# A Perceiver layer with 32 routed experts: six instead of eight experts with weights loaded ahead of routing, eight instead of seven blocks shared by 96 and 32 rows

## The chip, the cores and the metric

The kernel runs on one core of one Trainium2 chip. The time is device time in microseconds (us) of one execution of the whole program; lower is better. PE is the matrix engine (TensorE), DVE the vector engine, ACT the scalar engine, POOL is GpSimd, and SP the engine whose only work here is to issue DMAs. PEld is the loading of weights into PE. All arithmetic is in float32.

## The reference, cut to what matters

The layer takes 256 rows of 512 numbers and a context of 4096 rows, and adds three parts to the rows, one after the other: attention over the context (16 heads, 4 of keys and values), a state-space part with a convolution of width 4, and a mixture of experts. The last is what the change touches:

```python
x = hidden_states.reshape(-1, HID)                   # 256 x 512, layer-normed rows
scores = jax.nn.sigmoid(x @ gate_w)                  # 32 experts
topk_w, topk_i = jax.lax.top_k(scores, 6)
topk_w = topk_w / (jnp.sum(topk_w, axis=-1, keepdims=True) + 1e-20)
combine = jnp.sum(jax.nn.one_hot(topk_i, 32) * topk_w[..., None], axis=1)
g = jnp.einsum('td,edf->tef', x, wg)                 # wg, wu: 32 x 512 x 192
u = jnp.einsum('td,edf->tef', x, wu)
act = jax.nn.silu(g) * u
routed = jnp.einsum('tef,efd,te->td', act, wd, combine)   # wd: 32 x 192 x 512
shared = silu(hidden_states @ sg) * (hidden_states @ su) @ sd
return routed + shared
```

Each of the 256 rows is sent to 6 of 32 experts: 1536 pairs of row and expert, 48 for an expert in the mean. How many rows an expert really gets is known only when the program has run the first two parts and the router.

## The kernel before, in words

The program is written with a framework that puts instructions on the engines, finds dependences through tiles, and itself orders the instructions of each engine (a scheduler that knows estimated durations; `tc.issue_after(x)` holds instructions back until x). Attention and the state-space part come first and take about 780 us. What follows here is the expert part.

**Pairs and blocks.** The 32 experts are worked through in 16 pairs (`NP`, n = 0 to 15). A block is 128 rows for PE. A pair is of one of three kinds:

- n below `NW` (two blocks): each expert has a block of 128 rows of its own. `gate_up` (L1672 and on; its matmuls are in the helper at L237) makes gate and up for both with 16 matmuls, `turn_hidden` (L1690) transposes the hidden values (three transposes), and `down` (L1700, L1703) makes the result.
- the next `MIXED` pairs (one block): a large and a small expert share one block, 96 rows and 32 rows.
- the rest (one block): two experts share a block, 64 rows each.

For the one-block kinds `gate_up_two` (L1629) issues matmuls on column groups of 32 or 64 rows, each with the weights of the expert whose rows they are; `turn_hidden_two` (L1641) has two transposes and `down_two` or `down_here` (L1651, L1652) one result.

**Who gets which room.** The first `FIXED` experts keep their numbers: expert 2n and 2n+1 are pair n, whatever the routing says. The others are sorted by their count of rows on the chip, in `places` (L1250): the `WIDES` largest get full blocks, the next `MIXED` ones 96 rows, then come those with 64, and the smallest get 32 (tables made by `place_tables`, L1189). So for each place behind the fixed ones a table `place` says which expert sits there. If an expert has more rows than its room, `crowded` is 1 (`room`, L1341), and a long path (the Else branch behind L1818) computes all experts again in full; the short path only adds and stores the result.

**Weights.** An expert pair's weights are two tiles (gate, up and most of down) and a third with the rest of down, 2.36 MB together. There are `NHELD` = 6 places for a pair's weights in SBUF, made from tiles of the earlier parts as these come free (`hold`, L1420). Fixed pairs are loaded from `hold` as plain DMAs of SP, before routing (L1402 to L1407). The other pairs need `place`, so they are loaded after routing with indirect DMAs of POOL (L1394, called at L1410 to L1412), the first ones, up to pair 5, in this loop:

```python
for n in range(FIXED // 2, NHELD):
    with tc.issue_after(begun):
        begun = load_pair(n)
```

and pair n + 5 in round n, after `down(n - 1)` has freed its place.

**Rows.** The layer-normed rows lie in DRAM (`xd`). `fetch` (L1394 with `xg_sb`) gets a block's rows by an indirect DMA of POOL with the lists in `listed`; the lists of the first `EARLY` = 4 blocks are made ahead by `list_early`, those of the others by `list_later` (L1314, after gate and up of pair 0). `turn` transposes a block's rows on PE (L1601) and copies them on DVE (`xgT`, L1603).

**A round** n issues, in this order in the code: gate and up of n, fetches of blocks up to 4 ahead, `turn(n + 1)`, `down(n - 1)`, `load_pair(n + 5)`, `turn_hidden(n)`. In round 2 `weights_back` (L1716 to L1740) is called: a chain of some 40 small DVE instructions and ten transposes of PE (`spreadT`, L1739) that prepares the routing weights of the last `TAIL` = 10 experts. The results of the first pairs, up to n = 10, go to DRAM (`ye`) and are gathered again for each row (`yk`, 12 indirect DMAs) and added by DVE (L1565); those of the last five pairs are kept in SBUF and spread to their rows by PE (`total`, L1670).

The derived numbers, which the change moves:

```python
NW = (FIXED + WIDES) // 2
NSLOT = NE - FIXED
NB = FIXED + WIDES + (NSLOT - WIDES) // 2
NPL = NSLOT + NSLOT // 2
ZROW = (NW + LAST) * P
```

With FIXED = 8 and MIXED = 7 there are 5 pairs of two blocks (four fixed ones and the two largest of the rest), 7 of 96 and 32 rows, 4 of 64 and 64: NB = 21 blocks.

Of the kernel before, what the change touches and what calls it, by code (L numbers as in the profile page):

```python
# [53 lines left out]
WGU = KD * 2 * FE  # L54
WEX = WGU + DM
NHELD = 6
FIXED = 8
HALFP = P // 2
QUARTER = P // 4
WIDES = 2  # L60
MIXED = 7
HEAD = 4
EARLY = 4
TAIL = 10
NW = (FIXED + WIDES) // 2
LAST = NP - TAIL // 2
# [3 lines that stand above are left out]
# [4 lines left out]
def first_rows(n):  # L74
    return P - QUARTER if n < NW + MIXED else HALFP

# [8 lines left out]
def perceiver_layer(ctx: ExitStack, tc: tile.TileContext, a: dict, out: bass.AP):  # L85
# [64 lines left out]
    def layer(ctx, bounded):  # L150
# [1024 lines left out]
        def routing_memory():  # L1175
# [9 lines left out]
            V.tensor_scalar(m["free"], ident[:, 0:NE], 1.0, None, ALU.mult)  # L1185
            V.memset(m["free"][:, 0:FIXED], 0.0)
            V.tensor_tensor(m["before"], upper, ident, ALU.subtract)

        def place_tables():  # L1189
# [4 lines left out]
            def steps(to, first, *by):  # L1194
                to = to if len(by) == 1 else to.rearrange("p (a b) -> p a b", b=by[1][1])
                G.iota(to, pattern=[list(b) for b in by], base=first, channel_multiplier=0, allow_small_or_imprecise_dtypes=True)

            turn, rows, room, w = m["turn"], m["table"][:, 0], m["table"][:, 1], WIDES + 2 * MIXED
            for to, at0, step, more, narrow in ((turn, 0, 1, NSLOT - MIXED - WIDES, 1), (rows, FIXED * P, P, P - QUARTER, HALFP)):
                steps(to[:, 0:WIDES], at0, (step, WIDES))  # L1200
                steps(to[:, WIDES:w], at0 + WIDES * step, (step, MIXED), (more, 2))
                steps(to[:, w:NSLOT], at0 + (WIDES + MIXED) * step, (narrow, NSLOT - w))
            steps(room[:, WIDES:w], QUARTER, (0, MIXED), (P - HALFP, 2))
            V.tensor_scalar(rows[:, NSLOT:], m["p"], float(P), None, ALU.mult)
# [45 lines left out]
        def places(pc):  # L1250

            pos, key, keys, at, value, drawn = (
                m[n] for n in ("pos", "key", "keys", "at", "value", "dst"))
            n, low = NSLOT, slice(FIXED, NE)
            two = lambda ap, k: ap.unsqueeze(1).to_broadcast([P, 2, k])
# [655 lines left out]
```

## Time and profile before

| | us |
|---|---|
| three timed runs | 940.9, 940.94, 943.85 |
| their median | 940.94 |
| the profiled execution | 946.23 |
| its span, from first to last instruction | 944.3 |
| first fetch of rows (POOL) | 801.85 |
| first gate and up matmuls (pair 0) | 810.04 |
| last instruction group of PE (`total`) ends | 937.9 |

The page of a profile gives the busy time of each engine, then the span in 40 slices, DMA queues, and the chain of work that ended last: followed back from the last instruction, at each step to whatever released it. The share of an engine in that chain says how much of the time hangs on it. Answers of the trace give single rows: start, duration, engine, line, operation, the tiles, and in brackets how long the engine had been idle and who released it. "Landed" is the time at which a DMA's semaphore is counted up. The granted clock of PE is 1.00 where PE runs at full speed; the mean of this execution is 0.997.

### The profile page before, as it was taken

What the parts mean: (1) busy time and instruction counts of PE and PEld (TensorE: products, weight loads), DVE (VectorE), ACT (ScalarE), POOL (GpSimd) and SP (SyncE); (2) the same over time, 40 slices, a digit from 0 to 9 for tenths busy, and PEclk for the clock granted to TensorE, in tenths of its full rate; (3) what the DMA queues carried; (4) which work ended last, traced back from release to release, by engine and by line L of the source; (5) the groups of instructions that cost most, each with busy time, mean ns of one, the idle gap of its engine ahead of it and who ended that gap; (6) DMA issues with size and microseconds to landing.
All of it is one profiled execution on the core that took longest, in us unless ns stands there. A gap on an engine that the chain in (4) does not pass through costs nothing.

```text
span 944.3 us, 10567 instructions
## 1 busy us (share of the span) xinstructions
PE 924.2 (98%) x3266; PEld 504.9 (53%) x3266; DVE 577.4 (61%) x1199; ACT 370.0 (39%) x853; POOL 427.8 (45%) x498
## 2 busy tenths in 40 slices
PE   7999999999999999999999999999999999999996
PEld 3444555555555555555555555554465775654332
DVE  4866766566666665756666656658588685661224
ACT  4556444344344343443444434434154442022121
POOL 3769846345544644724725544220013251545542
PEclk9999999999999999999999999999999999999999
DMA  9651053053024114204305203090025481779983
GB/s 331 203 112 58 1 179 89 1 154 92 1 66 146 33 31 159 57 3 154 90 0 157 68 1 89 14 298 1 0 101 197 145 309 68 288 287 348 421 330 101
DMA packets 129716, 122.33 MB, mean 130 GB/s; under 512 B 79889, under 2 KB 99122, under 8 KB 124402
## 3 DMA queue, kind: packets, MB, share of 16 engines
q1 hardware_dynamic: 118960, 77.43, 27.2%
q0 software_dynamic: 7504, 39.59, 11.3%
q10 hardware_dynamic: 3186, 4.54, 1.3%
q8 instruction: 28, 0.46, 0.2%
q14 instruction: 38, 0.31, 0.1%
HBM read 89.54 MB, written 32.00 MB: 129 GB/s over the span
## 4 chain that ended last, share of the span: by engine, by line
PE 96%; DVE 2%; DMA 0%; issue 0%; ACT 0%; POOL 0%; SPq 0%; ACTq 0%
PE oT L774 24%; PE scT L748 24%; PE ps_kv L522 16%; PE ps_self L237 4%; PE ps_egu L1629 3%; PE ps_o L969 3%; PE ps_egu L237 3%; PE ps_first L399 3%; PE ps_xbc L237 2%; PE ps_out L1163 1%; PE ps_z L237 1%; PE xgTp L1601 1%; PE ps_ye L1651 1%; PE ps_ye L1652 1%; PE total L1670 1%; PE ps_ye L1700 1%
## 5 line engine op out<-in xcount | busy, mean ns | idle before, releaser
L765 DVE TENSOR_TENSOR lacc<-lacc,prT 128x512 f32<-128x512 f32 x256 | 199.8, 781 | 198.0 <-ACT prT L754 196.6
L754 ACT ACTIVATE prT<-scT,bq,rk 128x512 f32<-128x512 f32 x256 | 198.4, 775 | 280.9 <-PE scT L748 268.8
L748 PE MATMUL scT<-qT,kT 128*128 128x512 f32 x536 | 273.5, 592 | 0.0
L774 PE MATMUL oT<-prT,v 128*128 128x512 f32 x528 | 269.4, 592 | 0.0
L774 PEld LDWEIGHTS oT<-prT,v 128*128 128x128 f32 x528 | 100.2, 190 | 125.3 <-issue 118.6
L748 PEld LDWEIGHTS scT<-qT,kT 128*128 128x128 f32 x536 | 101.3, 190 | 41.4 <-issue 30.8
L522 PE MATMUL ps_kv<-fast,ctx 128*128 128x256 f32 x350 | 99.5, 379 | 0.0
L522 PEld LDWEIGHTS ps_kv<-fast,ctx 128*128 128x128 f32 x350 | 66.5, 190 | 47.9 <-issue 39.9
L471 POOL TENSOR_TENSOR ctx<-ctx 128x128 f32<-128x128 f32 x21 | 10.4, 495 | 98.7 <-PE ps_kv L522 98.7
L211 POOL TENSOR_TENSOR rk<-pv,mhalf 128x4 f32<-128x4 f32 x32 | 38.7, 1219 | 27.3 <-DVE pv L210 27.1
L522 PE MATMUL ps_kv<-wkv,ctx 128*128 128x256 f32 x168 | 48.8, 379 | 0.0
L282 ACT ACTIVATE xn<-kraw 128x128 f32<-128x128 f32 x112 | 33.5, 301 | 38.5 <-POOL kraw L497 21.5
L507 POOL TENSOR_TENSOR v<-fast,v 128x768 f32<-128x768 f32 x21 | 40.8, 1958 | 16.5 <-DVE fast L551 15.9
L522 PEld LDWEIGHTS ps_kv<-wkv,ctx 128*128 128x128 f32 x168 | 31.9, 190 | 28.2 <-issue 24.6
L780 DVE TENSOR_TENSOR oacc<-oT,oacc 128x512 f32<-128x512 f32 x64 | 43.7, 682 | 0.0
L1394 POOL DMA_INDIRECT xg_sb<-xd,listed x21 | 20.1, 959 | 31.7 <-DVE lacc L1258 14.4
L522 PE MATMUL ps_kv<-fast,fast 128*128 128x256 f32 x112 | 33.3, 379 | 0.0
L1633 DVE TENSOR_TENSOR hid<-si,ps_egu 128x128 f32<-128x128 f32 x11 | 3.2, 288 | 47.0 <-ACT si L1631 40.0
L522 PEld LDWEIGHTS ps_kv<-fast,fast 128*128 128x128 f32 x112 | 21.3, 190 | 17.8 <-issue 12.0
L288 DVE STREAM_TRANSPOSE tr<-kraw 128x512 f32<-128x512 f32 x28 | 18.3, 690 | 19.6 <-POOL kraw L496 19.6
L469 POOL TENSOR_TENSOR ctx<-fast 128x128 f32<-128x128 f32 x28 | 20.4, 730 | 19.6 <-PE ps_kv L522 19.1
L969 PE MATMUL ps_o<-wo,qT 128*128 128x512 f32 x64 | 28.8, 592 | 0.0
(423 smaller groups left out, 1399.9 us busy)
## 6 DMA issues: line engine op xcount, KB each, us to landing
xg<-xn SPq DMA_DIRECT2D x6, 2560.0 KB
ctx<-in_ctxT_dram SPq DMA_DIRECT2D x7, 1024.0 KB, 4.7
kd<-tr SPq DMA_DIRECT2D x112, 64.0 KB, 2.2
kT<-kd SPq DMA_DIRECT2D x28, 256.0 KB, 2.8
wq<-in_wq_dram SPq DMA_DIRECT2D x4, 1024.0 KB, 10.4
wo<-in_wo_dram SPq DMA_DIRECT2D x4, 1024.0 KB
w_in<-in_W_inT_dram SPq DMA_DIRECT2D x4, 1024.0 KB, 11.7
w_in<-in_experts_dram SPq DMA_DIRECT2D x4, 1024.0 KB, 6.9
```

What stands on the lines that cost most here:

```text
L211: return G.tensor_tensor(dst, v[:, :n], mhalf[:, :n], ALU.pow)
L237: last = TE.matmul(ps, lhs(k), rhs_of(k), start=(k == 0), stop=(k == KD - 1))
L282: S.activation(sq[:, h, :], raw[:, h, :], AF.Square, accum_out=ss[:, h:h + 1])
L399: TE.matmul(ps, lhs[:, j, k, :], rhs[:, k, :], start=(start and k == 0), stop=(k == 1), skip_group_check=True)
L507: G.tensor_tensor(to[:, 1:4], q, base[:, 1:4], ALU.add)
L522: TE.matmul(b[n], sets[name][i], y, start=start, stop=True, skip_group_check=True)
L748: scored.append(TE.matmul(sc, kT[:, g, i * P:(i + 1) * P], qT[:, t, heads4(g), :].rearrange("p h q -> p (h q)"), start=True, stop=True).ins)
L754: S.activation(pr, sc, AF.Exp, bias=shift, scale=SCALE if r is None else r[:, i, g:g + 1])
L765: V.tensor_tensor(la, la, pr, ALU.add)
L774: TE.matmul(outs[g, t], v[:, i, g * HD:(g + 1) * HD], pr, start=(n == 0), stop=last)
L780: V.tensor_tensor(ov, outs.pop((g, t)), ov, ALU.add)
L969: TE.matmul(m["ps_o", t], aT[:, t, h, :], wo[j][:, h % 4, :], start=(h == 0), stop=(h == NH - 1))
```

## The change

Two constants change, and with them the derived ones.

```diff
-FIXED = 8
+FIXED = 6
 HALFP = P // 2
 QUARTER = P // 4
 WIDES = 2
-MIXED = 7
+MIXED = 8
```

Experts 0 to 5 (pairs 0 to 2) have their weights loaded ahead of routing; experts 6 and 7 join those that are sorted by count. Pair 3 is now that of the two largest of the rest, with two blocks, and its weights are loaded by three indirect DMAs of POOL after routing, ahead of those of pairs 4 and 5. Pairs 4 to 11 are of 96 and 32 rows, pairs 12 to 15 of 64 and 64 as before. `NW` goes from 5 to 4, `NSLOT` from 24 to 26, `NPL` from 36 to 39 and `NB` from 21 to 20. The same six places hold the weights, and the last five pairs are still the ones kept in SBUF.

## The prediction before the run

> **What bounds the kernel now.** I read the busy times first, then the chain of work that ended last, then DMA in the page's slices.
>
> ```profile
> PE 924.2 (98%) x3266; PEld 504.9 (53%) x3266; DVE 577.4 (61%) x1199; ACT 370.0 (39%) x853; POOL 427.8 (45%) x498
> DMA  9651053053024114204305203090025481779983
> PE 96%; DVE 2%; DMA 0%; issue 0%; ACT 0%; POOL 0%; SPq 0%; ACTq 0%
> ```
>
> PE is busy 98% of the span and is 96% of the chain, so the time is that of PE's instruction stream plus the places where it has to wait. DMA is idle in most of the span and full only in slices 35 to 39, which is the expert part. The change touches only that part, so I looked at it in stretches of 10 us (busy time and count of PE, PEld, DVE, ACT, POOL; then PE's granted clock, DMA share, GB/s):
>
> ```profile
> 800.00:810.00 10.00, 8.53 (x41) 5.15 (x39) 7.51 (x34) 0.56 (x3) 5.88 (x6) 1.00 0.39 112
> 810.00:820.00 10.00, 9.96 (x52) 7.84 (x53) 6.43 (x24) 0.70 (x3) 4.94 (x6) 0.93 1.00 409
> 820.00:830.00 10.00, 10.00 (x31) 5.21 (x31) 6.11 (x17) 1.69 (x4) 5.75 (x9) 0.90 0.54 179
> 830.00:840.00 10.00, 10.00 (x37) 5.29 (x37) 8.11 (x28) 1.63 (x4) 3.91 (x5) 1.00 0.86 324
> ...
> 870.00:880.00 10.00, 9.40 (x76) 3.32 (x78) 2.67 (x8) 2.48 (x6) 5.61 (x6) 1.00 1.03 425
> ```
>
> From 870 to 910 DMA runs at 416 to 425 GB/s, share 1.01 to 1.03: it has nothing to spare there. At 820 it is half free. PE still sets the end, but transfers stand close behind: the rows of pair 14 land 3.75 us before their transposes, those of pair 15 4.2 us (landings at 907.7 and 914.5; uses at 911.4 and 918.75).
>
> Last, the chain itself, for two neighbouring pairs (start, us, what): gate_up(4) of two full blocks, then gate_up(5), the first of one shared block.
>
> ```profile
> 847.67 0.87 PE xgTp L1601 x8
> 848.55 1.72 PE ps_ye L1700 x4
> 850.26 1.06 PE ps_ye L1703 x4
> 851.33 0.48 PE hidTp L1690 x3
> 851.80 5.16 PE ps_egu L237 x16
> ...
> 863.37 0.59 PE xgTp L1601 x4
> ...
> 866.74 0.37 PE hidTp L1641 x2
> 867.11 2.72 PE ps_egu L1629 x32
> 869.83 0.58 PE xgTp L1601 x4
> 870.41 1.00 PE ps_ye L1651 x8
> ```
>
> The two prices of a pair can be read here.
>
> **The change, part by part.**
>
> *Routing.* Counting the reference's routing on its own inputs, sorted rooms hold every expert: the largest counts outside experts 0 to 5 are 103 and 88 (rooms of 128), then 74 to 63 in the eight rooms of 96, 55 to 34 in those of 64, and 26 to 1 in the eight of 32; experts 0 to 5 hold at most 100. So the short path is taken, before and after. The list has 16 columns in place of 17, the placement matmul 26 in place of 24: each such instruction costs as before within hundredths. Cost 0.
>
> *One pair fewer of two blocks, one more of one block.* PE, two blocks: 0.87 + 1.72 + 1.06 + 0.48 + 5.16 = 9.29 us. One block: xgTp 0.59, hidTp 0.37, gate and up 2.72, down 1.00 + 1.06 (the row of the same matmuls at 871.41) = 5.74. Saving 3.55 us, all on the chain: PE is busy 10.00 of 10 us from 850 to 870. The other engines lose work too (one xgT copy of 0.69, one silu, one y copy); none is on the chain and I cost them at nothing. POOL loses one row fetch of 0.95 us.
>
> *Pair 3's weights move.* Three SP transfers (2.36 MB) leave the time before routing, where DMA is idle anyway (share 0.00 at 790 to 800). They are queued on SP ahead of nothing that PE waits for: the xd store behind them goes out at 788.11 when its rows are written, and the first fetch waits until 801.85 for DVE, not for that store. Gain 0. They return as three indirect loads at the head of POOL's row at 807.75. Each is 0.95 us plus 0.30 between, 3.75 in all. POOL idles 3.61 us there:
>
> ```profile
> 813.98 0.95 POOL L1394 DMA_INDIRECT oacc<-in_down_rest_dram,place  x1 [0.30 <-issue]
> 818.54 0.95 POOL L1394 DMA_INDIRECT xg_sb<-xd,listed  x1 [3.61 <-DVE lacc L1343]
> ```
>
> So issuing costs 0.1 to 0.4 us on rows that are not yet wanted. Queued behind them on POOL are the weights of pairs 4 and 5 (wanted 30 us later), then rows of pairs 2 and 3. The transfer itself is 2.36 MB at 409 GB/s, 5.8 us; before, the six loads end at 822.15, so now near 828, and the rows of pair 2, which landed at 824.1 and 824.7, come at about 830 to 831. They were wanted at 828.91.
>
> *The order around it.* In the built program the scheduler answers this: on PE, hidTp(1) and down(1) come ahead of xgTp(2); on DVE, the whole chain of weights_back (L1718 to L1737) comes ahead of the two xgT(2) copies, which in the profile before stand in its middle:
>
> ```profile
> 829.63 1.28 DVE L1603 COPY xgT<-xgTp 128x512 f32<-128x512 f32 x2
> 831.47 5.16 PE ps_egu L237 x16
> ```
>
> That chain runs from 826.93 to 836.65, with 1.28 of xgT, and two hid pairs of about 0.4 inside it: 8 us of its own, so it ends near 835. One copy (0.69) later, gate_up(2) starts near 835.8, against 831.47: 4.3 late. Down(1), 1.72 + 1.06 = 2.78, is then already done, and 0.3 of transposes. So gate_up(3) starts 1.2 us late (near 843.0, against 841.89). PE idles in two pieces, some 0.8 us before down(1), for hidT(1), and 1.9 us before gate_up(2). From below: if weights_back is interrupted by nothing and the copies slip in, 0; from above: 2.7, the two idles. I take 1.2, the walk. After gate_up(3) nothing differs until the tail but one block fewer, so gate_up(6) starts 3.55 − 1.2 = 2.35 us early.
>
> *The tail.* Gathers of finished rows and adds start when pair 10's row store has landed, so they move with PE. But PE and DVE are ordered anew from gate_up(12) on: two adds (0.75 us each, L1565) now stand between hid(15) and its last half, before the last hidTp, where there was none. Two matmuls of totals (0.86 for two) fill part. From 0 to +1.5; I take +0.8.
>
> *Late releases.* After gate_up(7) to (10), silu (L1631) starts 2.1, 1.5, 1.9 and 0.6 us after the modelled end of its matmuls, and PE waits for it: rounds take 6.2 to 6.7 rather than 5.6 to 5.9 us. Nothing in the trace says why, so whether the new mixed round gets such a delay is open: −2 to +2; taken as 0, since the cause isn't seen to change.
>
> *The clock.* Granted clock was 0.93 and 0.90 in 810 to 830, which cost 0.7 + 1.0 = 1.7 us, after PE had idled 1.47 us in 800 to 810. New idles at 829 and 834 may bring a second such stretch: 0 to +1.7. [...]
>
> **Sum:** −3.55 + 1.2 + 0.8 = −1.55 us. The profiled execution took 946.23 us (span 944.3) and would take 944.7; it lies 5.3 above the median of 940.94, with nothing in its page to tell why, and I apply the difference to the median: 939.4.
>
> **Rivals.**
>
> *The whole block is kept* (−3.55, or −4 with a late release fewer): 937.2. For it: the scheduler's order costs nothing if xg(2) and weights_back are done sooner than in my walk. Against: DVE is busy 8.11 of 10 us at 830 to 840.
>
> *Transfers become the bound: slower, 943.5.* After routing, DMA moves 2.36 MB more and 0.52 less (one block of rows in and out): 1.84 MB, 4.4 us at 420 GB/s. Place: 830 to 914, POOL's loads waiting for eight earlier ones, then PE for xg(14) and xg(15). If the hole at 820 to 830 takes it (0.46 of 10 us = 4.6), DMA's end stays near 914.5. If it doesn't, the last rows come 4.4 to 5.6 later, near 920; PE, 2.35 early, would want them at 916.4, and stalls 2.5 to 3.7, which eats the saving, and the tail and a slow clock after the stall come on top (0.8 + 1.7): +0.2 to +4, middle +2.5. It decides from the point where the end of transfers moves by more than 4.2 − 2.35 = 1.85 us. Against: slots come free with down(1) 4 to 8 us sooner, so loads of pair 7 start sooner. [...]
>
> *Reordering and a second slow stretch*: −3.55 + 2.7 + 0.8 + 1.7 = +1.65: 942.6.
>
> *It does not do what it says*: an expert overflows its room and the long path runs, 32 half passes of 9.29 us, about 297 us more. Excluded by the counts.
>
> **How the numbers follow.** Forecast 939.4, chance 0.37; whole block kept 0.22; transfers 0.23; reordering and clock 0.17; overflow 0.01. About 0.3%, 2.8 us, is what a measurement of this kernel can tell from no change: faster means under 938.1, slower over 943.8. Whole block kept gives 0.19 faster and 0.03 same; the forecast, whose open terms spread it to 937 to 942 and at the ends beyond, 0.14 faster, 0.20 same, 0.03 slower; transfers 0.09 same, 0.14 slower; reordering 0.10 same, 0.07 slower; overflow 0.01 slower. Together faster 0.33, same 0.42, slower 0.25. The range goes from 935.5 (whole block kept and some 2 us of late releases gone) to 946.0 (transfers' upper end of 945 with a late release more); the forecast's own is 937 to 942.
>
> **What would show it.** gate_up(4) has L1629's form and lasts 2.7 us; PE's sum falls by 3 to 4 us. DMA share at 820 to 830 rises from 0.54 to 0.9 or more. gate_up(3) starts 1.2 us later, gate_up(6) some 2.3 us sooner than before. PE idles near 829 and 834, and the clock in 830 to 850 tells of a second slow stretch. xgTp(14) and (15) wait for DVE or nothing; if they wait for DMA, the transfers' rival holds. The forecast is wrong if weights_back does not hold up xgT(2), if late releases change by more than 2 us, or if the two executions differ ahead of 800 us.

## The result and the profile after

The changed kernel is **slower**: median 953.08 us in 14 runs (951.78 to 954.7), against 942.65 us in 14 runs of the kernel before (940.9 to 950.27), a ratio of 1.0101 [1.0085, 1.0117]; the two medians alone give 1.0111. The forecast was 939.4 us, with a range from 935.5 to 946.0. The profiled execution after took 954.19 us with a span of 952.3, before it was 944.3: 8.0 of the 10.4 us can be followed in the two traces. The other 2.4 come from the execution of before that was profiled, which lies 3.6 us above the median of its 14 runs, where that of after lies 1.1 above its own.

First the page of after: busy times, granted clock, DMA, and the chain's shares.

```profile
PE 926.9 (97%) x3279; PEld 503.2 (53%) x3279; DVE 579.0 (61%) x1197; ACT 369.2 (39%) x851; POOL 429.7 (45%) x500
PEclk9999999999999999999999999999999999899997
DMA  9651053053034024104305203360046441879962
PE 0%; DVE 0%; issue 0%
```

PE has a block less to do and is busy 2.7 us longer. The clock row has an 8 in slice 35 and a 7 in the last. The chain is no help: followed back from the end, it breaks off after three pieces, so the stretches must be read instead. Those of 10 us (busy time and count of PE, PEld, DVE, ACT, POOL; granted clock, DMA share, GB/s):

```profile
810.00:820.00 10.00, 8.71 (x46) 6.35 (x46) 5.47 (x20) 0.66 (x2) 6.90 (x8) 0.96 0.98 394
820.00:830.00 10.00, 8.73 (x23) 5.42 (x24) 4.30 (x12) 1.14 (x3) 4.88 (x8) 0.70 1.00 406
830.00:840.00 10.00, 7.81 (x29) 3.32 (x28) 9.45 (x31) 2.73 (x5) 4.60 (x5) 1.00 0.74 257
```

From 810 to 840 PE was busy 29.96 of 30 us before; now it is busy 25.25, and its clock between 820 and 830 is 0.70 instead of 0.90. DMA between 820 and 830 has no room left (1.00, from 0.54), as forecast.

To place the loss I cut both traces at the same events. x0 is the first fetch of rows, so that differences ahead of the expert part drop out.

| us | before | after | difference | forecast |
|---|---|---|---|---|
| x0 | 801.85 | 802.20 | +0.35 | 0 |
| x0 to the start of gate_up(6) | 65.19 | 66.43 | +1.24 | −2.35 |
| to the start of gate_up(12) | 36.07 | 35.68 | −0.39 | 0 |
| the tail: to the last write of x_sb (L1811) | 35.51 | 42.20 | +6.69 | +0.8 |
| from there to the end of the span | 5.68 | 5.79 | +0.11 | 0 |

Two rows are wrong: the head by 3.6 us, the tail by 5.9.

**The head.** The list of rows for blocks 4 and on, `listed`, is cast on DVE when PE has made it in PSUM (`ps_list`, L1314). Before, then after (start, duration; in brackets how long the engine idled, and what released it):

```profile
818.09 0.18 DVE L1315 CAST listed<-ps_list 128x17 uint32<-128x17 f32 x1 [1.80 <-PE ps_list L1314]
```

```profile
821.04 0.17 DVE L1315 CAST listed<-ps_list 128x16 uint32<-128x16 f32 x1 [4.40 <-remote]
...
821.27 1.11 PE L1601 MATMUL xgTp<-ident,xg_sb 128*128 128x128 f32 x4 [2.17 <-DVE listed L1315]
```

The cast is 2.6 us later, counted from the start of gate_up(0) (10.65 against 8.05), and PE stands still for 2.17 us behind it. The matmuls themselves had ended in time, at 818.41; what came late, at 821.02, is the event by which PE releases DVE. "remote" says that the profile has no instruction to put it down to. In the same stretch the clock was at half for 6.83 us (before: 3.41, from 818.51), in the first half of which PE was mostly idle:

```profile
819.24:822.65 3.41, 1.38 (x6) 1.38 (x7) 1.18 (x5) 0.02 (x1) 0.95 (x1) 0.50 1.01 416
822.65:826.06 3.41, 3.41 (x6) 1.76 (x6) 2.68 (x5) 0.46 (x1) 2.98 (x6) 0.50 1.02 423
```

**The tail.** Six buffers `yk` hold gathered rows until an add (L1565) has used them. POOL's gathers, before and then after:

```profile
919.64 1.41 POOL L1557 DMA_INDIRECT yk<-ye,row_y  x1 [0.30 <-issue]
...
926.83 0.95 POOL L1557 DMA_INDIRECT yk<-ye,row_y  x1 [0.30 <-issue]
```

```profile
919.77 0.95 POOL L1557 DMA_INDIRECT yk<-ye,row_y  x1 [0.30 <-issue]
926.67 0.94 POOL L1557 DMA_INDIRECT yk<-ye,row_y  x1 [5.96 <-DVE x_sb L1565]
930.74 1.34 POOL L1557 DMA_INDIRECT yk<-ye,row_y  x1 [3.12 <-DVE x_sb L1565]
...
936.66 1.17 POOL L1557 DMA_INDIRECT yk<-ye,row_y  x1 [0.30 <-issue]
```

Before, the twelve follow one another without a wait for a buffer. After, the seventh waits 5.96 us for DVE's first add, the eighth 3.12 for the second. DVE shows why. Its first add before, and its rows after:

```profile
915.26 0.75 DVE L1565 SCALAR_TENSOR_TENSOR x_sb<-yk,lacc,x_sb 128x512 f32<-128x512 f32 x1 [1.91 <-DMA yk<-ye,row_y]
```

```profile
925.65 0.75 DVE L1565 SCALAR_TENSOR_TENSOR x_sb<-yk,lacc,x_sb 128x512 f32<-128x512 f32 x1
...
929.72 4.56 DVE L1565 SCALAR_TENSOR_TENSOR x_sb<-yk,lacc,x_sb 128x512 f32<-128x512 f32 x6
934.33 0.29 DVE L1633 TENSOR_TENSOR hid<-si,ps_egu 128x128 f32<-128x128 f32 x1
...
936.26 0.75 DVE L1565 SCALAR_TENSOR_TENSOR x_sb<-yk,lacc,x_sb 128x512 f32<-128x512 f32 x1 [0.73 <-DMA yk<-ye,row_y]
937.04 0.22 DVE L1635 TENSOR_TENSOR hid<-si,ps_egu 64x64 f32<-64x64 f32 x1
```

In the new order of DVE the first add stands behind the products of hid(14), which wait for PE, though its rows landed at 916.72, 8.9 us sooner. Six adds then run in one piece, and the last halves of hid(15) stand behind an add whose rows, gathered late, have only just landed. PE pays at the end; before, then after:

```profile
912.01 1.08 PE L1651 MATMUL ps_ye<-w_in,hidT 128*64 128x512 f32 x4
```

```profile
918.04 1.07 PE L1651 MATMUL ps_ye<-lacc,hidT 128*64 128x512 f32 x2
919.05 0.66 PE L1601 MATMUL xgTp<-ident,xg_sb 128*128 128x128 f32 x4
919.63 1.07 PE L1651 MATMUL ps_ye<-w_in,hidT 128*64 128x512 f32 x2
...
937.32 0.33 PE L1641 MATMUL hidTp<-ident,hid 128*128 128x128 f32 x1 [1.43 <-DVE hid L1635]
...
939.38 2.08 PE L1652 MATMUL ps_ye<-v,hidT 128*128 128x512 f32 x2
```

The last row is two matmuls that took 1.12 before: the clock is at half, from 938.70 to 945.53. The first rows show a second loss. The four matmuls of a down on two column groups took 1.08 us when they stood together; now two of one group stand on either side of `xgTp`, and each two take 1.07. In these rows two groups took no longer than one (1.08 against 1.07) where their matmuls were neighbours, and twice as long where they were apart.

### The profile page after: what moved, and what is told of

It is laid out like the page before. It is cut to its first block, busy times and chain, and to the rows that moved or that the text cites. A ratio compares the mean times of both kernels' runs of the same rounds, so it can differ in the third digit from the quotient of the medians.

```text
span 952.3 us, 10576 instructions
## 1 busy us (share of the span) xinstructions
PE 926.9 (97%) x3279; PEld 503.2 (53%) x3279; DVE 579.0 (61%) x1197; ACT 369.2 (39%) x851; POOL 429.7 (45%) x500
## 5 line engine op out<-in xcount | busy, mean ns | idle before, releaser
L471 POOL TENSOR_TENSOR ctx<-ctx 128x128 f32<-128x128 f32 x21 | 10.4, 496 | 98.7 <-PE ps_kv L522 98.7
```

## The experiments

The theory that I held, A in the texts below (A2 after the first four kernels), puts the loss on *order*, not on amounts of work: three more indirect loads in POOL's row ahead of the list make the list late, and the scheduler's new order of DVE and PE makes the tail late. The rivals are a bound of transfers, the clock by itself, and late events that have nothing to do with the order. Beside the times I give stretches of each trace, cut as above: *list* (cast of `listed` from the start of gate_up(0)), *g6* and *g12* (x0 to the start of gate_up(6) and (12)), *tail* (gate_up(12) to the last write of x_sb), *end* (from there to the end of the span). Each ratio is to runs of before taken beside that kernel; their medians were 942.99 (e1 to e4), 940.37 (e5 to e8), 942.06 (f1 to f4) and 943.54 (g1), so medians of different groups are not to be compared directly.

| kernel | list | g6 | g12 | tail | end | median | ratio to before |
|---|---|---|---|---|---|---|---|
| before | 8.05 | 65.19 | 101.26 | 35.51 | 5.68 | 942.65 | |
| after | 10.65 | 66.43 | 102.11 | 42.20 | 5.79 | 953.08 | 1.0101 [1.0085, 1.0117] |
| e1 move alone | 10.76 | 70.33 | 105.99 | 33.45 | 8.29 | 951.35 | 1.0074 [1.0044, 1.0103] |
| e2 block alone | 8.05 | 61.49 | 97.25 | 33.45 | 7.89 | 941.82 | 0.9978 [0.9962, 0.9995] |
| e3 tail as before | 10.71 | 66.63 | 101.70 | 34.96 | 5.67 | 950.64 | 1.0061 [1.003, 1.0092] |
| e4 tail and head | 10.77 | 66.94 | 102.42 | 33.69 | 6.44 | 947.06 | 1.0047 [1.0021, 1.0073] |
| e5 block and tail | 8.05 | 60.11 | 93.55 | 33.57 | 5.62 | 936.82 | 0.9958 [0.9944, 0.9972] |
| e6 pair 5 later and tail | 8.05 | 61.22 | 95.12 | 33.31 | 5.70 | 938.34 | 0.9977 [0.9968, 0.9987] |
| e7 adds alone | 8.05 | 63.81 | 97.25 | 33.92 | 6.50 | 941.61 | 1.0013 [1.0004, 1.0023] |
| e8 adds as before | 8.05 | 61.43 | 94.87 | 37.32 | 5.67 | 942.18 | 1.002 [1.001, 1.0029] |
| f1 after again | 10.59 | 65.43 | 100.28 | 41.98 | 5.69 | 952.03 | 1.0109 [1.0092, 1.0126] |
| f2 = e8 again | 10.54 | 65.87 | 100.78 | 37.33 | 5.70 | 947.18 | 1.0054 [1.0037, 1.0071] |
| f3 = e6 again | 8.05 | 62.73 | 98.05 | 33.31 | 6.75 | 940.74 | 0.9979 [0.9969, 0.999] |
| f4 = e3 again | 10.50 | 65.46 | 100.31 | 34.90 | 5.74 | 949.5 | 1.0091 [1.0074, 1.0107] |
| g1 pair 5 alone | 8.05 | 62.78 | 98.94 | 44.95 | 5.02 | 951.79 | 1.0088 [1.0071, 1.0105] |

**The two halves of the change.** e1 moves pair 3's weights and keeps 21 blocks; it is the kernel before with

```diff
-FIXED = 8
+FIXED = 6
-WIDES = 2
+WIDES = 4
```

> FIXED 6, WIDES 4, MIXED 7: the weights of pair 3 move behind routing, but there are 21 blocks of rows as before (five pairs of two blocks, seven of 96 and 32, four of 64 and 64). Its head is ordered as in the changed kernel; its tail on PE is nearly that of before, its adds on DVE stand as in the changed kernel. Theory A (the loss is 3.4 us at the list of rows and the slow clock near 820, 1.2 from the reordered head, and the rest from the reordered tail; transfers only start it): 3.4 + 1.2 + 2 to 4 of the tail = 6.6 to 8.6 above before, 949 to 951. Theory B (transfers bound the rounds from 830 on): more bytes than the changed kernel, so at least as slow, 953 to 957. Theory C (the shape of pairs matters, not the move): as before, 942 to 943.

Measured: 951.35 us. The move alone costs nearly all of it. g12 is 4.7 us above before's: 2.7 for the late list, 1.3 for the order around it (measured below); the 0.7 left is about what the half clock can have cost more than in before (6.83 us with PE busy 5.32, against 3.42 us with PE busy throughout). The tail up to x_sb is short (33.45), but the span ends 8.29 us after it. The adds are late here as well (the first at 925.38), so the last gather goes out at 934.55, and the span ends 15.55 us after it, at 950.1. Over all traces the span ended 5.6 to 5.8 us after the last write of x_sb (5.0 in g1), or, where that distance is longer (e1, e2, e4, e7, f3), 15.1 to 15.7 us after the last gather. In after the two fall together: 936.66 + 15.64 and 946.51 + 5.79 both give 952.3.

e2 has the 20 blocks, but SP loads pair 3's weights ahead of routing as before (those of experts 6 and 7, whatever the routing says):

```diff
+EARLYW = 4
-return load_weights(weights[n], n, 2 * n < FIXED, behind)
+return load_weights(weights[n], n, n < EARLYW, behind)
-if len(held) % 2 == 0 and len(held) <= FIXED:
+if len(held) % 2 == 0 and len(held) <= 2 * EARLYW:
-for n in range(FIXED // 2, NHELD):
+for n in range(EARLYW, NHELD):
```

> The changed kernel, but pair 3's weights are loaded by SP ahead of routing, as fixed ones: the block is saved and nothing moves. Pair 3 then works with the weights of experts 6 and 7 in place of the two that its rows were sent to, so that its part of the result is another one; the instructions and their sizes are those of the changed kernel. Its head is ordered as before, its PE tail nearly as before, its adds on DVE as in the changed kernel. Theory A: -3.55 and +2 to 4 for the adds, 941 to 943. Theory B: the block's saving whole, 939. Theory C: 950 or more, since the shapes are those of the changed kernel.

Measured: 941.82 us, 0.9978. The list is on time and g6 is 3.7 us below before's. The gain is partly lost at the end (7.89): the adds are ordered late here too.

**The tail.** e3 is the changed kernel with adds and PE held in the order of before from pair 12 on. `tc.issue_after` ties gate_up(14) behind the first add and turn(15) behind the fourth, and chains PE's stages:

```diff
-gate_up(n)
+with held_by(TE, n > LAST + 1), tc.issue_after(adds[0]) if n == NP - 2 else nullcontext(): gate_up(n)
-main.turn(n + 1)
+with held_by(TE, n > LAST), tc.issue_after(adds[3]) if n == NP - 2 else nullcontext(): main.turn(n + 1)
-main.down_here(n - 1)
+with held_by(TE, n < NP - 1): main.down_here(n - 1)
```

(`spread_last` and `turn_hidden` likewise.)

> The changed kernel with the tail of PE (from gate_up(12) on) and the adds on DVE held to the order of before, by issue order alone, no new waits. Theory A: the tail's 6.7 us go back to about 0: 946 to 948. Theory B: the waits are for transfers and come back elsewhere: 951 to 954.

Measured: a tail of 34.96 us, 7.2 below after's, but a median of 950.64, with runs from 945.13 to 954.04. They follow the mean granted clock: 945.13 and 945.43 at 0.996 and 0.997, 954.04 at 0.991; 0.006 of 945 us is 5.7 us of the 8.6 between them. The traced execution is one of the shorter ones (947.1). At a mean clock of 0.995 or 0.996 three runs of e3 took 945.1 to 947.5, where those of after took 951.8 to 952.9; at 0.991 both took over 952. So the order of the tail shows in the trace, and most executions lose the gain again at a lower clock; in which stretch, their times don't tell.

e4 is e3 with weights_back held behind the copies of xgT(2) (`with tc.issue_after(turned[n - 1])` in place of `main.done[n - 1]`).

> As the third kernel, and weights_back on DVE is held behind the two copies of xgT(2), so that gate_up(2) does not wait for it. Theory A: 0 to 1.5 us below the third kernel, 945 to 947, since down(1) already fills most of that wait and spreadT now comes later into gate_up(3). If the chain on DVE was the costly wait of the head: 3 to 4 us below the third kernel, 943 to 944.

Measured: 947.06, 1.0047 [1.0021, 1.0073]; its interval overlaps that of e3. gate_up(3) starts 43.78 us after x0, against 44.51, but gate_up(6) no earlier (66.94, against 66.63). Inconclusive in time: the order of weights_back is worth 0.7 us at most, and nothing of it is left at gate_up(6).

e8 and f2 hold only the adds (`adds[0]` and `adds[3]` of e3's diff) and leave PE to the scheduler; f1, f2, f3 and f4 ran together on one chip.

> The changed kernel with the adds on DVE ordered as before, and PE's tail left as the scheduler orders it (halves of ps_ye apart from each other, sums moved forward). Theory A2: the head's 4.5 less the block's 3.55 and what PE's split costs, 1 to 3 us; gathers end early: 946 to 949. Rival (the whole tail is PE's order): as the changed kernel, 952 to 953.

> The changed kernel unaltered, beside the next three on one chip. In the last four traces no release of PE was late and the clock stayed at 1.00 from 815 on, in the earlier ones it was 0.50 around 820 to 825: this run tells how much of the 10 us belongs to that. Theory D (late releases and the slow clock come with the moment, the orders of head and tail with the kernel): where the list of rows is released 8.05 us after gate_up(0) and the clock stays at 1.00, 943 to 947 against 940.4 for before (as the run with its adds put back, 942.2, plus 1 to 5 for the adds); where the list is late and the clock falls, 952 to 954 as at first. Theory A: 952 or more in both.

> The changed kernel with the adds as before, a second time. Theory D: where the list is not late, 942; where it is late, 3 to 5 us more, 945 to 948.

> The tail of PE and DVE as before, a second time. It took 945 to 954 in ten runs. Theory D: where the list is not late, 938 to 941, a little above the kernel with pair 5's loads later, for the reordered head; where it is late, 945 to 952 again.

e8 took 942.18, under its 946 to 949: its list was on time (8.05) and its clock stayed at 1.00 up to the last write of x_sb. So its head shows the new order around pair 2 by itself. From e7, which has before's order there, gate_up(2) goes from 28.07 to 32.37 us after x0, and PE waits twice:

```profile
829.69 1.13 PE L1700 MATMUL ps_ye<-lacc,hidT 128*128 128x512 f32 x2 [1.58 <-ACT hidT L1692]
834.31 2.85 PE L237 MATMUL ps_egu<-w_in,xgT 128*128 128x384 f32 x8 [0.55 <-DVE xgT L1603]
```

f1's list was late (10.59), so its 952.03 fits both theories. Measured tails: 41.98 (f1), 37.33 (f2), 34.90 (f4). So the adds' order costs 4.65 us of the tail. In f1 the clock was at half for 6.83 us ahead of the last write of x_sb, with PE busy for 5.88 of them, so some 2.9 of the 4.65 are the half clock; of all traces only after, f1 and g1 show a fall there. PE's order costs 2.4 from f2 to f4, and 3.75 from e8 to e5, which differ in the loads too. The split down of pair 13 accounts for 1.07 of that; the halves of pair 14's down lie beside matmuls of gate_up(15) in f2 and cost 0.3 there (3.86 us from the first of both to the start of L1652, against 3.59 in before; in after and f1 both splits stand around `xgTp`). In time, f1 to f2 is 4.85 us. f2 to f4 shows no gain (947.18 and 949.5): f4's traced execution is its fastest (943.9, at 0.997), the others go up to 951.19 at 0.992. PE's 2.4 thus rests on the traces of undisturbed tails alone, and that holding PE's order shortens the median is not shown by this pair.

e7 goes the other way: the kernel before with the first add put behind hid(14) and the next behind the copies of xgT(15), PE's order left as it was.

```diff
-main.turn(n + 1)
+copied = main.turn(n + 1)
-add_behind(n, *{NP - 3: (0, TOPK), NP - 2: (TOPK, 2 * TOPK - 2), ...
+add_behind(n, *{NP - 3: (0, 0), NP - 2: (1, 2 * TOPK - 2, copied), ...
```

> The kernel before, with one thing of the changed one: the first add of gathered rows stands on DVE behind hid(14), the next ones behind xgT(15). Theory A2: gathers 7 to 12 wait for the six buffers that the adds free, the last one is issued about 4 to 6 us later, POOL closes the program late: 3 to 4 us slower, 946 to 947. Rival (only PE's order and the head cost anything): 942 to 943.5.

Measured: 941.61, only 1.2 us above the 940.37 of before, far under what was expected. The order of DVE alone is cheap: 1.2 us here, and 2.2 to 2.6 us at the ends of e1 and e2, whose PE tails are nearly before's. It becomes dear together with PE's new order, in which hid(14) and xgT(15) come later.

**The head.** e5 is e2 with the tail held. It has the block's saving and neither loss.

> The second kernel (block saved, pair 3's weights loaded by SP ahead of routing, so pair 3 works with the weights of experts 6 and 7) with the tail's order of before on PE and DVE. In the second kernel x_sb was done at 933.4, 5.2 earlier than before, but POOL, whose last gather of yk was issued at 926.16 and which is done 14.4 later, closed the program at 940.5. Theory A2 (the end is the later of two: x_sb plus 4.9, and the last gather plus 14.4; adds that come late on DVE hold the gathers): gathers end some 4 us earlier, x_sb sets the end, 2 to 2.5 us below the second kernel: 939.5. Rival (POOL's close does not hang on the gathers): as the second kernel, 941.8.

Measured: 936.82, 0.9958. This bounds what the block is worth. e6 and f3 keep the change and the held tail and put only six loads on POOL ahead of the list, by holding pair 5's three back until the rows of pair 2 have been fetched:

```diff
-for n in range(FIXED // 2, NHELD):
+for n in range(FIXED // 2, NHELD - 1):
...
+with tc.issue_after(begun): begun = load_pair(NHELD - 1) if n == 0 else begun
```

> The changed kernel with the tail's order of before, and pair 5's three loads issued on POOL behind the fetches of pair 2's rows, so that six loads and not nine stand in DMA's queue when the list of rows is made. The scheduler then orders the head as before. Theory A2 (the loads ahead of routing's list cause the late release of the list, the slow clock and the late rows): gate_up(1) starts 9.7 us after gate_up(0), as before, and not 12.0 to 12.2; time 939 to 941. Rival B (transfers bound the rounds from 830 on, whatever their order): late waits for DMA in the later rounds, 947 to 951.

> Pair 5's loads later and the tail as before, a second time. If the nine loads ahead of the list cause its late release, this kernel keeps 8.05 us even where the others are late, 939 to 941; if they have nothing to do with it, it is late like the others, 942 to 945. Where no kernel is late: 938.

Measured: 938.34 and 940.74, 0.9977 and 0.9979: **faster than both kernels**, on two occasions. f3's list, and its gathers:

```profile
818.13 0.17 DVE L1315 CAST listed<-ps_list 128x16 uint32<-128x16 f32 x1 [1.80 <-PE ps_list L1314]
```

```profile
914.76 0.95 POOL L1557 DMA_INDIRECT yk<-ye,row_y  x1 [0.30 <-issue]
...
924.32 1.29 POOL L1557 DMA_INDIRECT yk<-ye,row_y  x1 [0.30 <-issue]
```

The list is on time; the seventh gather waits for nothing, the eighth for 3.10 us, and the last goes out 12.3 us sooner than after's. f4 differs from f3 in pair 5's loads alone and ran on the same chip: 949.5 against 940.74.

g1 has f3's head with the tail left to the scheduler.

> The changed kernel with pair 5's three loads behind the fetches of pair 2's rows, and the tail as the scheduler orders it: nothing is held there. Its head is that of the kernel with pair 5's loads later (list 8.05 us after gate_up(0), gate_up(3) some 40 to 41 us after the first fetch), its tail on PE is again apart in halves, its first add stands on DVE behind hid(14). If head and tail cost each for itself: the head's 2.3 to 3.5 come back and the tail's 6.5 stay, 947 to 950 beside 952 of the changed kernel. If the tail suffers only because the head is late: 940 to 942.

Measured: 951.79. g12 is 2.3 us below before's, and the tail is 44.95: its seventh gather waits 8.36 us for an add, its eighth 3.75, and the clock is at half for 10.24 us of the tail. That is above both ranges of the expectation: the 3.2 us that g12 gains on after's are lost again in a tail 2.75 us longer. So curing the head leaves the tail's loss, and curing the tail (e3, f4) leaves the head's; either keeps the kernel slower than before. The two do not simply add in the medians: beside f1's 952.03, the tail alone (f4) gains 2.5 us, both (f3) 11.3, and the head alone nothing clear (ratios 1.0088 of g1, 1.0109 of f1). The traced executions of f4 and f3 differ by 2.1 us only (943.9 and 941.79); the rest of the 8.8 between their medians lies in executions without a trace, with mean clocks of 0.992 to 0.995 in f4 and 0.997 to 0.999 in f3. At which places the clock fell there is not shown.

## Where the prediction was right and where it failed

- **The block (−3.55): right.** e7 has before's head and e5 the head with a block less; both ran on one chip with PE's clock at 1.00 there. g6 falls from 63.81 to 60.11: 3.7 us. gate_up(4) has L1629's form and took 2.79. (The row at 867.11, from which its 2.72 was read, is gate_up(6); gate_up(5), at 860.66, took the same 2.72.)
- **The order around it (+1.2): right in size, not in its wait.** From e5 to e8, which moves the loads, g6 rises by 1.32, and gate_up(2) is 4.3 late as forecast. But the waits are 1.58 us before down(1), for hidT(1), and 0.55 before gate_up(2), where I had 0.8 and 1.9: hidTp(1) and down(1) ahead of xgTp(2) on PE make the delay, and weights_back holds up xgT(2) very little. With its chain behind the copies (e4), PE still waits 0.35 us before gate_up(2), against 0.62 in e3. That the sum came out is partly luck. The head's sum was forecast as −2.35; from e7 to e8 it is −2.38, since e8's list happened to be on time.
- **Late releases ("taken as 0") failed in size.** The list came 2.6 us late, and the whole head with it: in f1, whose clock was at half no longer than before's, g6 is 65.43 − 65.19 = +0.24, and 0.24 + 2.35 is 2.6. I had looked for such delays at gate_up(7) to (10), bounded them by 2, and did not ask which release stands ahead of the head's chain. What makes it late stays **open**. It goes with the count of loads: with nine on POOL ahead of the list it was late in 7 of 8 traces, with six in none of 7. But e8 has nine, and its list was on time. Two of PE's events reached DVE almost together: in after, those for `ps_list` and `xgTp`, at 821.02 and 821.08, though the matmuls had ended at 818.41 and 818.89.
- **The clock (0 in the sum, bound 1.7)**: no run shows the 0. The clock makes most of the 1.0 that is left of the head's 3.6: in after it was at half for 6.83 us there, in which PE was busy 1.38 + 3.41, in before for 3.41; half of what is busy is taken as excess, 2.4 against 1.7, an estimate from the two matmuls that took 2.08 at half and 1.12 before. Another 6.83 us at half are part of the tail's loss. I had put the fall in before down to PE's idle 1.47 us in 800 to 810; the 3.41 us right ahead of the fall held no idle time (last section).
- **The tail (+0.8, "from 0 to +1.5") failed worst**: +6.7. The false sentence is that gathers and adds "move with PE". That holds for gathers 1 to 6, which have buffers. The seventh and those behind it need a buffer that an add has freed, and adds stand in the order of DVE. I had seen two adds ahead of hid(15)'s last half and priced them by their durations (0.75 each), not by what they wait for: an add that waits for a gather, which waits for an add behind hid(14). I also read only which instructions changed places on PE, and not that this took two column groups apart (2 × 1.07 in after). f1 to f2 shows 4.65 us for the adds' order, f2 to f4 2.4 for PE's.
- **Transfers (rival, 943.5): fell.** DMA filled the hole at 820 to 830 as forecast (share 1.00, from 0.54); the rows of pair 14 landed at 910.44 and were used at 919.05, those of pair 15 at 916.65 and 928.42. No transpose waited for them.
- **POOL's loads cost nothing on the rows they queue in**: right for pair 2, whose rows landed at 830.5 and 831.1 (forecast 830 to 831); `xgTp` used them at 837.35.
- **PE's sum "falls by 3 to 4"; it rose 2.7**: −3.55 for the block, +3.8 for the half clock (excess 5.5 us in head and tail, before 1.7) and +2.1 for the split downs make +2.35 of it.
- **What I carried over to the median** was the difference from one profiled execution, 5.3 us above the three runs shown. With 14 runs it lies 3.6 above.

The saving that was forecast exists, and the forecast gain of 1.55 us could be had: e6 and f3, 2.0 and 1.3 us below the runs of before beside them, are the change with an order that keeps it. What was wrong is that I took the new order of DVE and PE as a small disturbance of a tail bound by PE.

## What to carry to other kernels

An instruction that moves in an in-order row is priced by what it waits for and by who waits behind it, not by its duration; where a pool of buffers closes a ring (gather, add, free, gather), follow the ring once with the new order, up to the end of the program, which can hang on the last transfer rather than on the busiest engine (e1's span ended 15.55 us after its last gather). When a framework orders the instructions itself, two constants can change its order in places that the diff doesn't name: compare the orders of every engine, and hold a good one by hand. Matmuls on different column groups saved time here only as neighbours (1.08 us together, 2 × 1.07 apart).

## What the runs showed of the hardware

In the traces the granted clock was at half for 3.41 us (before, from 818.51), 6.83 (after, from 819.23 and from 938.70) or 10.24 (g1, in the tail), once, twice and three times 3.41, but for the last stretch of a trace, which the end of the program cuts. The two falls of after named here lie 119.47 us apart, 35 such steps. What came ahead of a fall was not always idleness. Two windows, one of before, then one of after (the columns are those of the stretches above):

```profile
815.10:818.51 3.41, 3.41 (x32) 3.28 (x31) 0.68 (x4) 0.33 (x1) 0.00 (x0) 1.00 1.04 432
```

```profile
935.29:938.70 3.41, 1.57 (x8) 0.38 (x6) 1.96 (x5) 0.43 (x2) 2.12 (x2) 1.00 0.65 183
```

In the first, PE's records leave no gap (busy 3.41 of 3.41 us), and the clock fell at 818.51 all the same; the window holds the 24 narrow matmuls of `ps_list` (17 columns each, 2.75 us together). It was the same in f3 and g1: PE was busy 5.00 of 5.00 us from 815 to 820, and the mean clock of these 5 us was 0.88 and 0.86. In e5 and e8, whose list was on time as well (8.05), there was no fall: PE was busy 4.93 of the same 5.00 us, at a clock of 1.00. In the second, PE idled 1.84 of 3.41 us, and the clock fell behind it, at 938.70. What sets these falls is not shown; that the narrow matmuls have a part in the first is a guess which no run here tested.
